# A graph-attention stack for 0/1 edges: softmax weights as products of factors, two graphs interleaved, the general code behind a branch

## Chip, cores, metric

One core of a Trainium2 chip. The metric is the device time of one launch in microseconds (us), the median of several runs; the runs of one kernel mostly agree within about 0.3%, the widest within 0.6%. A "graph" below is one of the 16 graphs of the batch, and the "period" is the time from the end of one graph's output to the end of the next one's. "Clock" is the mean granted TensorE clock of a stretch, as a share of full speed; in the clock records it is 1.00 or 0.50 at any one moment. An engine "stands" when it waits.

## The reference, cut to what matters

```python
# x [16, 1024, 256] float32; adj [16, 1024, 1024] int32 of 0 and 1, symmetric, with a full diagonal
def attend(h, adj, W, a, axis):                  # layers 0 (axis=1) and 1 (axis=-1)
    h = h @ W
    e = leaky_relu((h @ a1)[:, :, None] + (h @ a2)[:, None, :], 0.2)
    return elu(softmax(where(adj > 0, e, -BIG), axis) @ h)

def mean_messages(x, adj):                       # layer 2
    return relu(x @ W_upd + (adj.T @ (x @ W_msg)) / deg + bias)

def heads(x, adj):                               # layer 3: 4 heads of 64 columns
    h = x @ W                                    # per head
    for t in range(5):                           # edge types 1..5
        weight += (adj == t + 1) * (e_src[t][:, None] + e_dst[t][None, :])
    p = softmax(where(adj == 0, -BIG, leaky_relu(weight, 0.01)))
    return layernorm_per_head(relu(p @ h + bias) + h) * gamma + beta

for layer in (attend0, attend1, mean_messages, heads):
    x = x + layer(relu(layernorm(x)), adj)
```

The code allows edge types 1 to 5; the inputs hold only 0 and 1.

## The kernel before

It works on one graph at a time, layer after layer. Layer 3 builds each 128 x 1024 tile of logits from five candidates (one per edge type), takes a row maximum and the exponential, transposes the tile on TensorE, and multiplies.

```python
        def logits(item):                                  # layer 3, one head and one tile of rows
            h, i = item
            # ... kinds[i]: five uint8 masks, one per edge type (made anew for each pair of heads)
            nc.gpsimd.tensor_copy(w, base)
            for t in range(T):                             # T = 5
                nc.scalar.activation(e, ed_rows[h][:, t, :], AF.Identity, bias=hs[:, i, q : q + 1], scale=1.0)
                nc.vector.copy_predicated(w, kind[:, t, :], e)
            nc.vector.scalar_tensor_tensor(w, w, SLOPE3, w, op0=OP.mult, op1=OP.max)
            nc.vector.tensor_reduce(sc[:, 1:2], w, axis=AX.X, op=OP.max, negate=True)

        def attend(item, ready):
            rz = exp_sum(w, *ready)                        # exponential with row sum, on ACT
            pt = transposed(w)                             # 8 transposes on TensorE, 2 copies on ACT
            for n in range(NT):
                nc.tensor.matmul(ps[:, :HO], pt[:, n, :], hs[:, n, cols], start=(n == 0), stop=(n == NT - 1))
            # ... scaling, bias, relu, residual, statistics

    for b in range(B):                                     # one graph behind the other
        adj_n = layer0(b, xs, at); layer1(xs, adj_n); layer2(xs, adj_n)
        # ... next graph's x and first adjacency tiles are loaded here
        layer3(b, xs, adj_n)
```

Of the kernel before, what the change touches and what calls it, by code (L numbers as in the profile page):

```python
# [8 lines left out]
F32 = mybir.dt.float32  # L9
U8 = mybir.dt.uint8  # L10
AF = mybir.ActivationFunctionType
OP = mybir.AluOpType
AX = mybir.AxisListType

P = 128
#: Added to the logits of pairs that have no edge.
NO_EDGE = -1e30


@with_exitstack  # L20
def kernel(
    ctx: ExitStack,
    tc: tile.TileContext,
    x: bass.AP,
# [16 lines left out]
    beta3: bass.AP,  # L41
    out: bass.AP,
):
    """Four graph layers, one graph of the batch after the other, each on chip from its load to its store.

    adj_t is adj with its last two axes swapped; w*_t are the weights with the output axis first.
    a0, a1: [e, 2], the halves of the attention vectors as columns. w3: [d, (h e)]; w3_t: [e, h, d];
    a3: [e, h, 10], source then destination vectors of the five edge types.
    """
    nc = tc.nc  # L50
    B, N, D = x.shape
    NT = N // P
    DC = D // P
    HO, H, T2 = a3.shape
    T = T2 // 2
    HT = H * T
    HALF = 512
    NHALF = N // HALF
# [4 lines left out]
    const = ctx.enter_context(tc.tile_pool(name="const", bufs=1))  # L63
    dram = ctx.enter_context(tc.tile_pool(name="dram", bufs=2, space=bass.MemoryType.DRAM))
    wide_ps = ctx.enter_context(tc.tile_pool(name="wide_ps", bufs=2, space=bass.MemoryType.PSUM))
    tr_ps = ctx.enter_context(tc.tile_pool(name="tr_ps", bufs=2, space=bass.MemoryType.PSUM))
    mm_ps = ctx.enter_context(tc.tile_pool(name="mm_ps", bufs=2, space=bass.MemoryType.PSUM))

# [1 line left out]
    ident = const.tile([P, P], F32)  # L70
    make_identity(nc, ident)
    neg_half = const.tile([P, NT * H], F32)
# [4 lines left out]
        nc.sync.dma_start(t[:, :, :width], src.rearrange("(c p) f -> p c f", p=P))  # L77
        return t

    # Weights with W @ a in the columns behind them, so that one product gives both.  # L80
    wx0 = load_w(w0, D, "wx0", D + 2)
    wx1 = load_w(w1, D, "wx1", D + 2)
    wx2 = load_w(w2_msg, D, "wx2", 2 * D)
    nc.sync.dma_start(wx2[:, :, D:], w2_upd.rearrange("(c p) f -> p c f", p=P))
    wx3 = load_w(w3, D, "wx3", D + HT)
    wd3 = const.tile([P, DC, HT], F32)
    rows = {}
# [4 lines left out]
    with tc.tile_pool(name="prep", bufs=2) as prep:  # L92
        for wt, a, wx in ((w0_t, a0, wx0), (w1_t, a1, wx1)):
            wts = prep.tile([P, DC, D], F32, tag="prep_w", name="wts")
            nc.sync.dma_start(wts, wt.rearrange("(c p) f -> p c f", p=P))
            avs = prep.tile([P, DC, 2], F32, tag="prep_a", name="avs")
# [36 lines left out]
    next_x = load_x(0)  # L133
    next_at = [load_adj(adj_t, 0, n, "adj_t", AHEAD) for n in range(AHEAD)]

# [1 line left out]
    def inv_std(mv, n, eps):  # L137
        """(var + eps) ** -0.5 of n (mean, variance) pairs."""
        rs = small.tile([P, NT * H], F32, tag="rstd", name="rs")
        nc.vector.tensor_scalar(rs[:, :n], mv[:, :n, 1], eps, None, op0=OP.add)  # L140
        nc.gpsimd.tensor_tensor(rs[:, :n], rs[:, :n], neg_half[:, :n], op=OP.pow)  # L141
        return rs

    def norm_relu_t(xs):
        """relu(layernorm(x)), features on the partitions: [P, DC, N]."""
        mv = small.tile([P, NT * H, 2], F32, tag="mv", name="mv")
        for n in range(NT):
            st = small.tile([P, 6], F32, tag="bn", name="st")
            nc.vector.bn_stats(st, xs[:, n, :])
            nc.vector.bn_aggr(mv[:, n, :], st)  # L150
        rs = inv_std(mv, NT, 1e-5)
        ht = state.tile([P, DC, N], F32, name="ht")
        for g in range(NHALF):
            per = NT // NHALF
            pts = [tr_ps.tile([P, HALF], F32, tag="tr", name=f"pt_h{c}") for c in range(DC)]
            for k in range(per):
                n = g * per + k
                hn = work.tile([P, D], F32, name="hn")
                nc.vector.tensor_scalar(hn, xs[:, n, :], mv[:, n, 0:1], rs[:, n : n + 1], op0=OP.subtract, op1=OP.mult)  # L159
                for c in range(DC):  # L160
                    nc.tensor.transpose(pts[c][:, k * P : (k + 1) * P], hn[:, c * P : (c + 1) * P], ident)  # L161
            for c in range(DC):
                nc.scalar.activation(ht[:, c, g * HALF : (g + 1) * HALF], pts[c], AF.Relu)  # L163
        return ht

    def project(ht, wx, n, width):
        """Rows of one node tile times wx, in PSUM."""
        ps = mm_ps.tile([P, HALF], F32, tag="mm", name="ps_proj")
        for c in range(DC):
            nc.tensor.matmul(ps[:, :width], ht[:, c, n * P : (n + 1) * P], wx[:, c, :width], start=(c == 0), stop=(c == DC - 1))  # L170
        return ps
# [6 lines left out]
        return hs  # L178

    def row_everywhere(ht, wx, col):  # L180
        """h @ (W a) of all nodes along the free axis, the same on each partition (PSUM)."""
        ps = wide_ps.tile([P, N], F32, tag="wide", name="ps_row")
        for g in range(NHALF):
            for c in range(DC):
                nc.tensor.matmul(
                    ps[:, g * HALF : (g + 1) * HALF], wx[:, c, col : col + 1].to_broadcast([P, P]),
                    ht[:, c, g * HALF : (g + 1) * HALF], start=(c == 0), stop=(c == DC - 1),
                )
        return ps

    def pipelined(items, first, second):
        """second(item, first(item)) of each item, each behind the next item's first."""
        waiting = None
        for item in items:
            ahead = item, first(item)
            if waiting is not None:
                second(*waiting)
            waiting = ahead
        second(*waiting)

    def edge_logits(row, f, f_s, edges):
        """leaky_relu(row + f) where an edge is, and minus the largest in each row."""
        mask = work.tile([P, N], F32, tag="base", name="mask")
        nc.vector.tensor_scalar(mask, edges, 0.0, NO_EDGE, op0=OP.is_le, op1=OP.mult)
        y = work.tile([P, N], F32, tag="big", name="y", bufs=5)
        nc.scalar.activation(y, row, AF.Identity, bias=f_s, scale=SLOPE)  # L206
        nc.vector.scalar_tensor_tensor(y, row, f, y, op0=OP.add, op1=OP.max)  # L207
        sc = small.tile([P, 4], F32, tag="sc", name="sc", bufs=8)
        nc.vector.tensor_tensor_reduce(y, y, mask, 1.0, -3e38, OP.add, OP.max, sc[:, 0:1])  # L209
        nc.vector.tensor_scalar(sc[:, 1:2], sc[:, 0:1], -1.0, None, op0=OP.mult)  # L210
        return y, sc[:, 1:2], sc

    def exp_sum(out, y, neg_max, sc):
        """out = exp(y - max); returns 1 / its sum over each row."""
        nc.scalar.activation(out, y, AF.Exp, bias=neg_max, scale=1.0, accum_out=sc[:, 2:3])  # L215
        nc.vector.reciprocal(sc[:, 3:4], sc[:, 2:3])
        return sc[:, 3:4]

    def transposed(p):
        """[P, N] -> [P, NT, P]: each block of 128 columns transposed."""  # L220
        pt = work.tile([P, NT, P], F32, tag="big", name="p_t", bufs=5)
        per = HALF // P
        for g in range(NHALF):
            ps = tr_ps.tile([P, HALF], F32, tag="tr", name="ps_t")
            for k in range(per):
                n = g * per + k
                nc.tensor.transpose(ps[:, k * P : (k + 1) * P], p[:, n * P : (n + 1) * P], ident)  # L227
            nc.scalar.copy(pt[:, g * per : (g + 1) * per, :], ps.rearrange("p (k i) -> p k i", i=P))  # L228
        return pt

    def add_elu(v, xs):
        """xs += elu(v)."""
        e = work.tile([P, D], F32, name="e")
        nc.vector.tensor_scalar(e, v, 0.0, None, op0=OP.min)
        nc.scalar.activation(e, e, AF.Exp)
        nc.vector.scalar_tensor_tensor(xs, v, 0.0, xs, op0=OP.max, op1=OP.add)
        nc.vector.scalar_tensor_tensor(xs, e, -1.0, xs, op0=OP.add, op1=OP.add)

# [1 line left out]
    def layer0(b, xs, at):  # L240
        ht = norm_relu_t(xs)
        hs = gat_project(ht, wx0)
# [25 lines left out]
            add_elu(ps[:, :D], xs[:, i, :])  # L268
        return adj_n

# [1 line left out]
    def layer1(xs, adj_n):  # L272
        ht = norm_relu_t(xs)
        hs = gat_project(ht, wx1)
# [17 lines left out]

        pipelined(range(NT), logits, attend)

# [1 line left out]
    def layer2(xs, adj_n):  # L296
        ht = norm_relu_t(xs)
        hs = state.tile([P, NT, D + HT], F32, name="hs")
# [18 lines left out]
            nc.vector.scalar_tensor_tensor(v, ps[:, :D], sc[:, 2:3], up[:, j, :], op0=OP.mult, op1=OP.add)  # L317
            nc.vector.scalar_tensor_tensor(xs[:, j, :], v, 0.0, xs[:, j, :], op0=OP.max, op1=OP.add)

# [1 line left out]
    def layer3(b, xs, adj_n):  # L321
        ht = norm_relu_t(xs)
        # Destination terms of all heads and types, each spread over the partitions by way of DRAM.
        ed = work.tile([HT, N], F32, tag="big", name="ed", bufs=5)
        for g in range(NHALF):
            ps = mm_ps.tile([P, HALF], F32, tag="mm", name="ps_ed")
# [62 lines left out]
        for i in range(NT):  # L389
            for h in range(H):  # L390
                k = i * H + h
# [16 lines left out]
        layer3(b, xs, adj_n)  # L408


# [45 lines left out]
```

## Time and profile before

| before | value |
|---|---|
| time, median of 4 runs | 9663.72 us (9662.92 to 9665.43) |
| one graph | about 604 us, of which layer 3 some 380 |
| DVE busy | 7681 us, 79% of the span, 95% of layer 3 |
| TensorE busy | 5567 us, 58%, at a clock of 0.50 in layer 3 |

The table must be read by layer: DVE bounds layer 3, while layers 0 to 2 are a chain in which engines take turns. One more part of the page, the chain that ended last (shares of the span), says the same: TensorE and DVE share the end, and transfers hold 2% of it.

```profile
PE 42%; DVE 30%; issue 15%; ACT 9%; POOL 2%; DMA 2%; ACTq 0%; SPq 0%; DVEq 0%; POOLq 0%
```

### The profile page before, as it was taken

To read this page: it belongs to the slowest core of one execution; us is meant where nothing else is said; L and a number is where in the kernel's file an instruction comes from. 1 tells how busy PE (TensorE), PEld (TensorE's weight loads), DVE (VectorE), ACT (ScalarE), POOL (GpSimd) and SP (SyncE) were. 2 spreads that over 40 slices of the span, in tenths; PEclk is the share of its full clock that TensorE was granted. 3 is DMA by queue.
4 is the path that set the end of the run, shared out by engine and by line. 5 is a ranking of instruction groups with operands and counts; after the bars stand their busy time and mean duration, and the time that the engine had idled before them with its cause. 6 is when DMAs were issued, how large, how long until landed. Compare 5 with 4: busy or idle time off the path is not lost.

```text
span 9668.2 us, 73868 instructions
## 1 busy us (share of the span) xinstructions
PE 5566.9 (58%) x22944; PEld 4574.6 (47%) x22944; DVE 7681.3 (79%) x13109; ACT 5228.5 (54%) x6785; POOL 1194.6 (12%) x1238
## 2 busy tenths in 40 slices
PE   6456574565745647456475564755647556475564
PEld 5445454454544545445454454544545444454444
DVE  5977959779597795977959779597795977959778
ACT  2745727456374563745637456374563745637456
POOL 1110111101111011110111101011010110101101
PEclk8567585675856758566585665856658566585665
DMA  1110101101111011010110101101011010110000
GB/s 61 51 37 23 44 23 50 37 23 44 32 43 35 23 44 40 35 35 23 44 44 31 35 23 45 43 31 35 23 47 41 33 33 23 47 41 33 22 23 27
DMA packets 85208, 344.25 MB, mean 36 GB/s; under 512 B 8400, under 2 KB 43472, under 8 KB 76624
## 3 DMA queue, kind: packets, MB, share of 16 engines
q1 hardware_dynamic: 47952, 205.29, 5.7%
q0 software_dynamic: 36864, 134.23, 4.8%
q8 instruction: 185, 3.03, 0.1%
q14 instruction: 207, 1.70, 0.1%
HBM read 321.40 MB, written 18.09 MB: 35 GB/s over the span
## 4 chain that ended last, share of the span: by engine, by line
PE 42%; DVE 30%; issue 15%; ACT 9%; POOL 2%; DMA 2%; ACTq 0%; SPq 0%; DVEq 0%; POOLq 0%
PE ps_o L377 17%; PE ps_t L227 9%; DVE w L363 8%; ACT w L215 6%; DVE w L364 6%; DVE sc L366 5%; PE ps_o L288 5%; PE ps_o L264 4%; PE ps_proj L170 3%; DVE res L393 2%; DVE y L207 2%; POOL rs L141 2%; DVE y L209 2%; PE pt_h L161 2%; DMA ed_rows<-ed_d 2%
## 5 line engine op out<-in xcount | busy, mean ns | idle before, releaser
L363 DVE COPY_PREDICATED w<-kind,ps_e 128x1024 f32<-128x1024 uint8 x2560 | 3300.8, 1289 | 210.3 <-ACT ps_e L362 197.2
L362 ACT ACTIVATE ps_e<-ed_rows,hs 128x1024 f32<-128x1024 f32 x2560 | 2861.1, 1118 | 782.8 <-DVE w L363 705.7
L227 PE MATMUL ps_t<-ident,w 128*128 128x128 f32 x4096 | 1007.8, 427 | 2902.3 <-ACT w L215 2902.3
L227 PEld LDWEIGHTS ps_t<-ident,w 128*128 128x128 f32 x4096 | 803.1, 223 | 3002.0 <-ACT w L215 3002.0
L377 PE MATMUL ps_o<-hs,p_t 128*128 128x64 f32 x8192 | 1886.9, 425 | 12.3 <-ACT p_t L228 12.3
L377 PEld LDWEIGHTS ps_o<-hs,p_t 128*128 128x128 f32 x8192 | 1787.5, 330 | 156.7 <-ACT p_t L228 156.7
L215 ACT ACTIVATE w<-w,sc 128x1024 f32<-128x1024 f32 x512 | 587.9, 1148 | 789.9 <-DVE sc L366 789.9
L358 POOL COPY w<-base 128x1024 f32<-128x1024 f32 x512 | 574.2, 1125 | 3461.6 <-PE ps_t L227 3415.5
L163 ACT ACTIVATE ht<-pt_h 128x512 f32<-128x512 f32 x256 | 139.0, 594 | 1361.5 <-PE pt_h L161 1361.4
L354 DVE TENSOR_SCALAR kind<-adj 128x1024 uint8<-128x1024 f32 x1280 | 871.2, 685 | 0.0
L228 ACT COPY p_t<-ps_t 128x512 f32<-128x512 f32 x1280 | 741.9, 582 | 79.0 <-PE ps_t L227 26.3
L264 PE MATMUL ps_o<-hs,p_half 128*128 128x256 f32 x2048 | 570.8, 441 | 271.5 <-DVE sc L210 183.6
L161 PE MATMUL pt_h<-ident,hn 128*128 128x128 f32 x1024 | 295.9, 407 | 700.1 <-DVE hn L159 687.2
L170 PE MATMUL ps_proj<-wx,ht 128*128 128x258 f32 (+2 forms) x2048 | 664.6, 474 | 0.4
L264 PEld LDWEIGHTS ps_o<-hs,p_half 128*128 128x128 f32 x2048 | 439.8, 221 | 409.4 <-ACT y L206 200.5
L364 DVE SCALAR_TENSOR_TENSOR w<-w 128x1024 f32<-128x1024 f32 x512 | 627.1, 1225 | 0.5
L366 DVE TENSOR_REDUCE sc<-w 128x1 f32<-128x1024 f32 x512 | 615.9, 1203 | 0.5
L161 PEld LDWEIGHTS pt_h<-ident,hn 128*128 128x128 f32 x1024 | 168.4, 200 | 904.8 <-issue 637.2
L141 POOL TENSOR_TENSOR rs<-rs,neg_half 128x8 f32<-128x8 f32 (+1 forms) x80 | 192.7, 2409 | 2811.5 <-DVE rs L140 2811.5
L288 PE MATMUL ps_o<-hs,p_t 128*128 128x256 f32 x2048 | 492.8, 395 | 60.3 <-ACT p_t L228 60.3
L159 DVE TENSOR_SCALAR hn<-xs,mv,rs 128x256 f32<-128x256 f32 x512 | 264.5, 544 | 292.8 <-PE pt_h L161 177.4
L170 PEld LDWEIGHTS ps_proj<-wx,ht 128*128 128x128 f32 x2048 | 406.6, 209 | 163.3 <-issue 93.9
(72 smaller groups left out, 6082.8 us busy)
## 6 DMA issues: line engine op xcount, KB each, us to landing
ed_rows<-ed_d SPq DMA_DIRECT2D x64, 2560.0 KB, 8.8
adj_t<-in_adj_t POOLq DMA_DIRECT2D x128, 512.0 KB, 3.9
adj<-in_adj POOLq DMA_DIRECT2D x128, 512.0 KB, 3.9
xs<-in_x SPq DMA_DIRECT2D x16, 1024.0 KB, 5.9
out<-y SPq DMA_DIRECT2D x128, 128.0 KB, 1.7
ed_d<-ed SPq DMA_DIRECT2D x16, 80.0 KB
wx<-in_w SPq DMA_DIRECT2D x3, 256.0 KB, 3.6
wts<-in_w_t SPq DMA_DIRECT2D x2, 256.0 KB
```

Source lines behind the costliest of these rows:

```text
L170: nc.tensor.matmul(ps[:, :width], ht[:, c, n * P : (n + 1) * P], wx[:, c, :width], start=(c == 0), stop=(c == DC - 1))
L215: nc.scalar.activation(out, y, AF.Exp, bias=neg_max, scale=1.0, accum_out=sc[:, 2:3])
L227: nc.tensor.transpose(ps[:, k * P : (k + 1) * P], p[:, n * P : (n + 1) * P], ident)
L228: nc.scalar.copy(pt[:, g * per : (g + 1) * per, :], ps.rearrange("p (k i) -> p k i", i=P))
L264: nc.tensor.matmul(ps[:, :D], p_halves[n // per][:, n % per, i * P : (i + 1) * P], hs[:, n, :D], start=(n == 0), stop=(n == NT - 1),)
L288: nc.tensor.matmul(ps[:, :D], pt[:, n, :], hs[:, n, :D], start=(n == 0), stop=(n == NT - 1))
L354: nc.vector.tensor_scalar(kind[:, t, :], adj_n[i], float(t + 1), None, op0=OP.is_equal)
L362: nc.scalar.activation(e, ed_rows[h][:, t, :], AF.Identity, bias=hs[:, i, q : q + 1], scale=1.0)
L363: nc.vector.copy_predicated(w, kind[:, t, :], e)
L364: nc.vector.scalar_tensor_tensor(w, w, SLOPE3, w, op0=OP.mult, op1=OP.max)
L366: nc.vector.tensor_reduce(sc[:, 1:2], w, axis=AX.X, op=OP.max, negate=True)
L377: nc.tensor.matmul(ps[:, :HO], pt[:, n, :], hs[:, n, cols], start=(n == 0), stop=(n == NT - 1))
```

## The change

The intent has four parts.

1. Factors. With one edge type, exp(leaky(s + d)) = max(exp(s) exp(d), exp(a s) exp(a d)). Up to a factor that cancels in the softmax, one tile of weights is one DVE operation on a row and a column of exponentials and the 0/1 mask. No maximum, no wide exponential, no predicated copies.
2. Layout. The tile is made in the layout in which TensorE takes its weights, so the transposes of weights go. Row sums come from a column of ones in the product.
3. Layer 2 in float32r (a second 32-bit type for products), its messages split into a high part, which is the cast to that type, and a low part, which is what the cast leaves.
4. Two graphs interleaved. The code of a graph is a generator; a list orders the pieces of two graphs that stand 105 units apart (units are the numbers that the pieces yield in the code below). The engines take their queues in order, so this order decides what lies beside what.

A check at the end (sums of squares of the adjacency, sums of edges, size of the logit terms) decides by a branch whether the general code, which is the whole kernel before, runs as well.

```diff
-def tile_gnn_stack_kernel(
+def tile_general_stack(              # the whole kernel before, unchanged in what it does
 ...
+def tile_simple_stack(ctx, tc, flag, x, adj, adj_t, ...):
+    def layer3(b, xs, mask):
+        ht = norm_relu_t(xs)
+        # ... 8 projections into hs, logit terms into `terms`
+        yield 11
+        d_row = spread(column(terms[:, :, :H], H), H, (S3 - 1.0,), "l3")     # exp of terms -> DRAM
+        # ... q = exp((1 - S3) * terms); hb = (hs + bias) * exp(S3 * terms), on GpSimd
+        for h in range(H):
+            row = everywhere(d_row[h], "row3")                               # DRAM -> 128 partitions
+            for g in range(NHALF):
+                for j in range(NT):
+                    p = work.tile([P, HALF], F32, tag="p3", name="p3", bufs=14)
+                    nc.vector.scalar_tensor_tensor(
+                        p, row[:, half], q[:, j, h : h + 1], mask[:, j, half], op0=OP.max, op1=OP.mult)
+                    yield 0.2
+                for k in range(PER):
+                    for j in range(NT):
+                        nc.tensor.matmul(ps[:, k * HW : (k + 1) * HW],
+                            ps_[j][:, k * P : (k + 1) * P], hbv[:, j, h, :], start=(j == 0), stop=(j == NT - 1))
+                yield 5.4
+        for i in range(NT):
+            # ... normalisation per head on DVE, GpSimd (power) and ACT
+            nc.gpsimd.tensor_tensor(y, of, rows["gamma3"], op=OP.mult)
+            nc.gpsimd.tensor_tensor(y, y, rows["beta3"], op=OP.add)
+            nc.gpsimd.tensor_tensor(y, y, xs[:, i, :], op=OP.add)
+            nc.sync.dma_start(out[b, i * P : (i + 1) * P, :], y)
+            yield 0.5
+    # ... layers 0, 1, 2 in the same way; layer 0 makes a tile with two DVE operations
+    APART = 105.0
+    queue = [(b * APART, b, graph(b)) for b in range(B)]
+    while queue:                                   # the piece that is due first is emitted next
+        queue.sort(key=lambda g: g[:2])
+        at, b, g = queue.pop(0)
+        step = next(g, None)
+        if step is not None:
+            queue.append((at + step, b, g))
+    # ... the check, which counts what does not fit into `flag`
+    tile_simple_stack(tc, flag, *args)
+    again = nc.values_load(flag[0:1, 0:1], ...)
+    with tc.If(again > 0):
+        tile_general_stack(tc, *args)
```

## The prediction

> **What bounds the kernel now.** I read the page's totals first, then the slices, then busy time cut by layer for the first graph, then the costly groups, then single bursts in the timeline.
>
> ```profile
> PE 5566.9 (58%) x22944; PEld 4574.6 (47%) x22944; DVE 7681.3 (79%) x13109; ACT 5228.5 (54%) x6785; POOL 1194.6 (12%) x1238
> ...
> PE   6456574565745647456475564755647556475564
> ...
> DVE  5977959779597795977959779597795977959778
> ...
> PEclk8567585675856758566585665856658566585665
> ```
> DVE is the busiest engine, but its digits swing between 5 and 9: a mean over unlike layers. Busy us by engine in the layers of graph 0 (load, layers 0, 1, 2, start of 3, layer 3):
> ```profile
> 35.00:110.00 75.00, 52.51 (x184) 38.92 (x184) 50.15 (x117) 26.65 (x44) 14.78 (x15) 0.83 0.31 98
> 110.00:180.00 70.00, 53.80 (x250) 42.74 (x251) 43.21 (x101) 37.09 (x68) 1.64 (x1) 0.89 0.00 0
> 180.00:220.00 40.00, 39.44 (x143) 27.03 (x142) 16.09 (x49) 5.15 (x12) 0.00 (x0) 0.91 0.00 1
> 220.00:260.00 40.00, 23.73 (x91) 14.93 (x89) 17.09 (x36) 9.67 (x16) 4.71 (x4) 0.86 0.34 133
> 260.00:640.00 380.00, 180.16 (x778) 163.38 (x779) 361.67 (x533) 249.25 (x286) 62.96 (x65) 0.50 0.09 31
> ```
> Columns: stretch, length, PE, PEld, DVE, ACT, POOL, then the clock. Layer 3 takes some 380 of a graph's 604 us (9668/16); DVE is busy 95% of it and the clock is 0.50 because TensorE mostly waits. Layers 0 to 2 have no full engine but TensorE in layer 2: phases follow one another. The groups behind it:
> ```profile
> L363 DVE COPY_PREDICATED w<-kind,ps_e 128x1024 f32<-128x1024 uint8 x2560 | 3300.8, 1289 | 210.3 <-ACT ps_e L362 197.2
> L362 ACT ACTIVATE ps_e<-ed_rows,hs 128x1024 f32<-128x1024 f32 x2560 | 2861.1, 1118 | 782.8 <-DVE w L363 705.7
> ...
> L377 PE MATMUL ps_o<-hs,p_t 128*128 128x64 f32 x8192 | 1886.9, 425 | 12.3 <-ACT p_t L228 12.3
> ...
> L354 DVE TENSOR_SCALAR kind<-adj 128x1024 uint8<-128x1024 f32 x1280 | 871.2, 685 | 0.0
> ...
> L364 DVE SCALAR_TENSOR_TENSOR w<-w 128x1024 f32<-128x1024 f32 x512 | 627.1, 1225 | 0.5
> ```
> Five predicated copies per head and tile, one per edge type, make 43% of DVE's work. Bursts that give unit costs (transposes cold and warm, layer 3's products cold, layer 2's warm, two GpSimd rows):
> ```profile
> 429.65 1.97 PE L227 MATMUL ps_t<-ident,w 128*128 128x128 f32 x8 [5.36 <-ACT w L215]
> ```
> ```profile
> 139.10 1.04 PE L227 MATMUL ps_t<-ident,y 128*128 128x128 f32 x8
> ```
> ```profile
> 431.50 3.68 PE L377 MATMUL ps_o<-hs,p_t 128*128 128x64 f32 x16
> ```
> ```profile
> 199.54 27.90 PE L308 MATMUL ps_o<-hs,adj 128*128 128x257 f32 x128
> ```
> ```profile
> 618.03 0.73 POOL L395 TENSOR_TENSOR y<-res,row_gamma 128x256 f32<-128x256 f32 x1 [1.10 <-DVE res L393]
> ```
> ```profile
> 230.03 1.64 POOL L141 TENSOR_TENSOR rs<-rs,neg_half 128x8 f32<-128x8 f32 x1 [50.89 <-DVE rs L140]
> ```
>
> **What the Trainium skill says.** "TensorE: Matmul & The Clock Gate", section "What's actually happening", gives 1.2 GHz after idleness and 2.4 when busy; the trace agrees (clock 0.50 in layer 3; transposes 1.97 against 1.04). "FP8 and Floating Point Precision", "TensorE Precision Notes": true FP32 takes four passes. The trace agrees: a product shows as two records, and 128 records of 257 columns take 27.90 us, 0.218 each, two clocks per column. "VectorE: DVE Perf Modes", "Mode 2×_2P": fp32 tensor_scalar gets double rate, two-tensor operations do not; the trace agrees (685 ns against 1225 for 1024 elements). "Advanced Engine Details and Errata", "DVE Details" and "GPSIMD Details": the Pool engine shares an interface with DVE and conflicts when DVE has two SBUF inputs; nothing before isolates that. I found no page on float32r's rate.
>
> **The change, part by part.** With one edge type, exp(leaky(s+d)) is a maximum of two products of exponentials, so a tile of weights is one DVE operation (two in layer 0), already in the layout TensorE needs. All predicated copies, kind masks, row maxima, wide exponentials and transposes of weights go.
>
> TensorE per graph, full clock: 64 transposes x 0.107 (half of 1.97/8 = 0.246, less drain) = 7; projections, two of 258 columns (32 records x 0.218 = 7 each), one of 512 (32 x 0.43 = 14), one of 264 (7) = 35; layers 0 and 1, 128 records x 0.218 = 28 each. Layer 2 becomes 64 products with a high part and 64 with a low one in float32r: an estimate of one clock per column (0.108) gives 14. Layer 3 keeps 256 products, 512 records. Before, 16 took 3.68 less some 0.15 of drain, 0.22 each at half clock, set by the weight load (3.49 for 16); at full clock 0.107 to 0.11: 55. Sum 167 us, times 16 = 2,670.
>
> DVE per graph, consecutive operations starting about 0.08 earlier than durations suggest (1225 becomes 1.14): normalisations 32 x 0.39 + 1.5 = 14; layer 0 8 x 2.7 (two wide operations, reciprocal, scaling) + 16 x 0.38 = 28; layer 1 8 x 1.15 + 8 x 1.0 = 17; layer 2 16 x 0.42 + 8 x 1.15 = 16; layer 3 64 half-width x 0.62 = 40, output 8 x 1.95 = 16, copies and small ones 4. Sum 135, times 16 = 2,160, against 7,681. ACT about 70 a graph, GpSimd about 75. So TensorE becomes the fullest engine, but not alone.
>
> What interleaving hides I read from the queue orders of the built program, since each engine runs its queue in order. In a steady period (one graph), graph b ends layer 3 while b+1 ends layer 1; then b+1 does layer 2 with layer 0 of b+2; then b+1's layer 3 with b+2's layer 1.
> 1. Output of layer 3: on GpSimd eight rounds of three 256-wide operations (2.4 measured, 618.03 to 620.43) plus one power of four columns (about 1.0, by the slope from 1647 ns for 8 to 5457 for 32), plus mask loads: 30 us. On TensorE only 24 layer-1 products (10.4) lie beside it, and the last elementwise work of layer 1 is queued on DVE among this output. x has two buffers, so b+2's load waits for the end of the output.
> 2. Layer 2 projection, load and normalisation of b+2, its projection, row out to DRAM and back (about 7), then eight DVE rounds of 2.7 mixed with layer 2's ends (6): about 60 us from the output's end to the last weight tile, for 42 of TensorE work. Adjacency has 8 buffers for 16 half-tiles, so the second half loads behind the first half's products.
> 3. Then TensorE is full: 56 products of layer 0 (24), layer 3's projection (9), layer 3 (55), layer 1's projection (9), 40 products of layer 1 (17): 114.
> 4. Clock ramps after gaps and the start of layer 1's weights: about 7.
> Sum 211 us a graph. First output ends at about 360 (start 25, layers 0 and 1 nearly alone 140, then parts 2, 3, 1); 14 more periods, 2,954; last graph's layers 2 and 3 alone, and the check, about 150. That is 3,464. I place the prediction slightly lower, 3,400, as I counted some overlaps as serial.
>
> **Rivals.**
> - TensorE bound throughout, phase gaps hidden: 2,670 plus 100 to 150 for the ends, about 2,800. For it: two graphs have 334 us of TensorE work, more than one's own chain. Against it: in-order queues put both graphs' waiting phases (parts 1 and 2) side by side, and x's second buffer ties them.
> - DVE and GpSimd slow each other: almost every new DVE operation has two SBUF inputs. If GpSimd's 45 us of elementwise work per graph held DVE up for its length, the period would be 225 to 245 and the time 3,700 to 4,000.
> - float32r at FP32's rate: layer 2 takes 55 instead of 14, partly in part 2's slack: 20 to 40 a graph more, 3,750 to 4,050.
> - The check fails and the general code runs as well: about 13,000. Against it: adjacency is 0/1, symmetric, with a diagonal; degrees of at most 1024 are exact in both sums; the logit terms, sums of 256 products of order 0.1, should stay far under 30.
>
> **Range and chances.** All rivals but the last are at least twice as fast. 3,050 needs 20 us less a graph (output hidden, weight load at 0.09); 3,800 needs 25 more. Faster 0.985, same 0.005, slower 0.01.
>
> **What would show it.** Right: PE busy about 2,700 us, 78% of the span; DVE about 2,200; clock mostly 0.9 or more; layer-3 pairs at 0.11 us; dips of PE and full GpSimd once per period near 210 us; the longest TensorE waits in the transposes after layer 1 and in layer 0's products waiting for weights. Wrong: wide two-input DVE operations well over 1.2 us (port), 258-column float32r records near 0.2 or above, a clock near 0.5 in layer 3, or lines of the old code running after the check.

## The result, and the profile after

| | before | after |
|---|---|---|
| time, median of 4 runs each | 9663.72 us | 3831.82 us (3828.86 to 3833.42) |
| ratio | 1 | 0.3965 (0.3959 to 0.397) |

A ratio here is the mean time of one kernel's fast runs over that of the other's fast runs of the same rounds, so it is not quite the ratio of the medians.

The direction and the order of size are as predicted. The time is not: 3,832 us lies 432 us above the predicted 3,400 and 32 us above the top of the range. The page of the changed kernel, its totals and some of its slices:

```profile
PE 3033.8 (79%) x17490; PEld 2610.1 (68%) x17490; DVE 2277.1 (59%) x6389; ACT 1101.9 (29%) x2769; POOL 1059.5 (28%) x1366
...
PE   4778796877968778797877968779697877968785
...
POOL 1123314142132323214142132323314142132312
PEclk8899898989989889898888989899898989989865
```

DVE's work fell from 7,681 to 2,277 us, and TensorE is the fullest engine at 79%, close to the predicted 78%. But 79% of 3,830 us is 3,034 us of busy time, where 2,700 was predicted: work and time both came out an eighth larger, so the share agrees by luck. PE's dips still come once a period, and GpSimd is fullest in them. The last two digits of the clock, 6 and 5, are new: they come to matter below.

The groups that answer to the predicated copies of before, with busy time and mean of one:

```profile
L753 PE MATMUL ps_o<-hs,p 128*128 128x65 f32 x8192 | 1015.0, 286 | 107.4 <-DVE p L745 107.3
L745 DVE SCALAR_TENSOR_TENSOR p<-row,q,mask 128x512 f32<-128x512 f32 x1024 | 718.7, 759 | 358.1 <-PE ps_o L753 294.1
...
L559 PE MATMUL pt_h<-ident,hn 128*128 128x128 f32 x1024 | 206.1, 307 | 331.4 <-ACT hn L557 331.4
```

Layer 3's weights now cost DVE 719 us in all. The longest wait of TensorE is that of the transposes (331 us, most of it before layer 2, 18.3 a graph), as the prediction said; the wait for layer 3's first weights (107 us, 6.7 a graph) was not in its sum.

One period cut at the prediction's three parts. Columns: stretch, length, then busy time and count of PE, PEld, DVE, ACT, POOL, then the clock, DMA share and GB/s. The first line is part 1 (output of layer 3), then part 2 (to the last layer-0 weight tile), then part 3.

```profile
1513.30:1542.90 29.60, 11.30 (x52) 9.37 (x51) 21.14 (x98) 15.23 (x40) 25.36 (x30) 0.74 0.27 83
1542.90:1609.60 66.70, 50.13 (x221) 36.01 (x219) 36.80 (x103) 20.65 (x47) 9.11 (x15) 0.83 0.31 97
1609.60:1744.80 135.20, 124.75 (x818) 114.31 (x818) 83.36 (x198) 33.01 (x87) 31.35 (x41) 0.95 0.13 40
```

GpSimd fills 25.4 of part 1's 29.6 us; in part 3 TensorE is busy 92%. In part 2 nothing is full, which is the mark of a chain from engine to engine. The last GpSimd operation of the first graph's output and of the fifteenth's:

```profile
392.07 0.72 POOL L780 TENSOR_TENSOR y<-y,xs 128x256 f32<-128x256 f32 x1
```
```profile
3606.32 0.72 POOL L780 TENSOR_TENSOR y<-y,xs 128x256 f32<-128x256 f32 x1
```

(3,606.32 - 392.07) / 14 = 229.6 us a period, against 211. The prediction's own sum, before it was shaded, compares with the trace so:

| term of the sum | predicted | measured | excess |
|---|---|---|---|
| to the end of the first output | 360 | 393 | 33 |
| part 1 of a period | 30 | 29.6 | 0 |
| part 2 | 60 | 66.7 | 6.7 |
| part 3, ramps and start of layer 1 (114 + 7) | 121 | 135.2 | 14.2 |
| 14 periods (mean 229.6) | 2,954 | 3,214 | 260 |
| last graph alone, and the check | 150 | 223 | 73 |
| sum | 3,464 | 3,830 | 366 |
| shaded down to | 3,400 | | 64 more |

The three parts are those of the period shown, 231.5 us. Over twelve steady periods of the trace their means are 29.6, 64.9 and 135.2 us.

Three questions follow: what the last graph loses, what the 19 us a period are, and whether any rival (instruction cost of the branch, DVE and GpSimd on one port, float32r's rate) has a share in them.

### The profile page after: what moved, and what is told of

Same layout as the page of the kernel before. It is cut to its first block, busy times and chain, and to the rows that moved or that the text cites. A ratio compares the mean times of both kernels' runs of the same rounds, so it can differ in the third digit from the quotient of the medians.

```text
span 3829.6 us, 48243 instructions
## 1 busy us (share of the span) xinstructions
PE 3033.8 (79%) x17490; PEld 2610.1 (68%) x17490; DVE 2277.1 (59%) x6389; ACT 1101.9 (29%) x2769; POOL 1059.5 (28%) x1366
## 5 line engine op out<-in xcount | busy, mean ns | idle before, releaser
L753 PEld LDWEIGHTS ps_o<-hs,p 128*128 128x128 f32 x8192 | 1022.7, 204 | 128.3 <-issue 113.9
L753 PE MATMUL ps_o<-hs,p 128*128 128x65 f32 x8192 | 1015.0, 286 | 107.4 <-DVE p L745 107.3
L745 DVE SCALAR_TENSOR_TENSOR p<-row,q,mask 128x512 f32<-128x512 f32 x1024 | 718.7, 759 | 358.1 <-PE ps_o L753 294.1
L632 PE MATMUL ps_o<-hs,p 128*128 128x256 f32 x2048 | 529.9, 403 | 97.4 <-DVE hs L626 78.3
L665 PE MATMUL ps_o<-hs,p 128*128 128x257 f32 x2048 | 493.2, 399 | 40.4 <-DVE p L659 40.4
L632 PEld LDWEIGHTS ps_o<-hs,p 128*128 128x128 f32 x2048 | 389.5, 200 | 162.3 <-DVE hs L626 79.2
L665 PEld LDWEIGHTS ps_o<-hs,p 128*128 128x128 f32 x2048 | 398.2, 199 | 110.3 <-issue 54.9
L538 POOL TENSOR_TENSOR rs<-rs,neg_half 128x4 f32<-128x4 f32 (+1 forms) x192 | 238.6, 1244 | 835.3 <-DVE rs L537 817.0
L703 PE MATMUL ps_o<-hi,adj 128*128 128x258 f32 x1024 | 308.3, 329 | 121.9 <-DVE v L710 118.4
L557 ACT ACTIVATE hn<-xs,shift,rs 128x256 f32<-128x256 f32 x512 | 288.8, 598 | 217.7 <-DVE shift L550 167.0
L703 PEld LDWEIGHTS ps_o<-hi,adj 128*128 128x128 f32 x1024 | 230.9, 226 | 132.8 <-issue 127.8
L704 PE MATMUL ps_o<-lo,adj 128*128 128x258 f32 x1024 | 298.4, 320 | 0.0
L546 DVE BATCH_NORM_STATS2 st<-xs 128x6 f32<-128x256 f32 x512 | 204.7, 409 | 126.9 <-DMA xs<-in_x 123.8
```

Source lines behind the costliest of these rows:

```text
L538: nc.gpsimd.tensor_tensor(rs[:, :n], rs[:, :n], neg_half[:, :n], op=OP.pow)
L546: nc.vector.bn_stats(st, xs[:, n, :])
L557: nc.scalar.activation(hn, xs[:, n, :], AF.Relu, bias=shift[:, n : n + 1], scale=rs[:, n : n + 1])
L632: nc.tensor.matmul(ps[:, :D], ps_[j][:, i * P : (i + 1) * P], hs[:, j, :D], start=(j == 0), stop=(j == NT - 1))
L665: nc.tensor.matmul(ps[:, : D + 1], ps_[j][:, i * P : (i + 1) * P], hs[:, j, : D + 1], start=(j == 0), stop=(j == NT - 1),)
L703: nc.tensor.matmul(ps[:, : D + 2], a, hi[:, i, :], start=(i == 0), stop=False)
```

## The experiments

Where no other number is named, differences are against 3,831.8 us. Runs with two or four timings each.

### The branch and the general code behind it

```diff
-    with tc.If(again > 0):
-        tile_general_stack(tc, *args)
```

> The general code and its branch are left out; the 0/1 path alone runs. My theory (the time is sixteen in-order periods of about 230 us): 3,815 to 3,830 us, at most some 10 us less than the changed kernel, as nothing of the general code runs. Rival (the larger program costs time throughout, by instruction fetch): more than 40 us less.

Measured 3,827.67 us, 4 less, which lies within the spread of the runs. The code that isn't run costs nothing worth naming.

### The last graph's layer 3

In the tail TensorE is busy and slow at the same time. Windows of the kernel after: layer 3 of the last graph, then its output, then the check and the end.

```profile
3689.00:3787.00 98.00, 97.48 (x457) 97.30 (x457) 36.67 (x78) 3.56 (x10) 2.02 (x2) 0.50 0.03 12
3787.00:3818.00 31.00, 0.00 (x0) 0.00 (x0) 17.84 (x76) 10.82 (x31) 25.00 (x30) 0.50 0.09 31
3818.00:3830.00 12.00, 0.00 (x0) 0.00 (x0) 0.00 (x0) 0.00 (x0) 0.00 (x0) 0.50 0.04 14
```

For 98 us TensorE and its weight loads are busy 99%, yet the clock stands at 0.50, and 457 records take 0.214 us each. In a steady period the same products take 0.111. There, wide products of the other graph stand between them; here nothing does. If the clock is all that differs, then a few wide products ahead of the stream should lift it:

```diff
+        if b == B - 1:
+            for w in range(3):
+                ps = mm_ps.tile([P, HALF], F32, tag="mm", name="ps_warm")
+                for c in range(NT):                       # 128 x 512 products, result unused
+                    nc.tensor.matmul(ps, ht[:, 0, :P], ht[:, 0, :HALF], start=(c == 0), stop=(c == NT - 1))
         for h in range(H):
             row = everywhere(d_row[h], "row3")
```

> 24 extra 512-column FP32 products (result unused) before layer 3 of the last graph only. Theory (in the last graph layer 3's stream runs at half clock because it starts after a gap, and a stream bound by weight loads doesn't release the clock by itself): its 512 records go from 0.214 to 0.111 us and the span falls by 35 to 50 us, to about 3,785. Rival (such a stream can't hold the full clock): records back at 0.214 after a few us, span unchanged or up to 10 us longer.

Measured 3,789.33 us, 42 less. The trace of this run, a window inside the same stage and the run of products:

```profile
3690.00:3750.00 60.00, 58.12 (x516) 57.49 (x514) 37.96 (x82) 4.93 (x14) 2.42 (x3) 0.99 0.06 19
```
```profile
3706.14 41.98 PE L758 MATMUL ps_o<-hs,p 128*128 128x65 f32 x374
```

Same products, nearly the same busy share (97%), clock 0.99 in place of 0.50, 0.112 us a record (41.98 / 374) in place of 0.214. So the stream of narrow products, each with its own 128 columns of weights to load, stayed at the clock at which it began, high or low, for 40 to 100 us. This settles 42 us of the 73.

### One graph behind the other

```diff
-    APART = 105.0
+    APART = 1000.0
```

> Graphs one after the other instead of two interleaved, same operations. My theory: one graph alone takes about 135 us for layers 0 and 1 (25 to 160 us in the trace) and about 208 for layers 2 and 3 with its output (last graph), so 16 x 330 to 345 = 5,300 to 5,500 us; the factor form gives about 4,250 of the 5,830 us gained and the interleaving about 1,550. Rival (TensorE's work sets the time, interleaving matters little): below 4,300 us.

Measured 5,460.49 us. One period of it:

```profile
641.00:982.00 341.00, 248.53 (x1109) 216.12 (x1109) 148.96 (x402) 70.21 (x174) 65.89 (x85) 0.70 0.13 42
```

TensorE works 248.5 us a graph here, against 186.2 in the period of the interleaved kernel shown above, for the same products. The clock is 0.70, and layer 3 is at half speed in every graph. To see how much of interleaving's gain is filled gaps and how much is the clock, the same serial kernel got 16 wide products ahead of every layer 3:

```diff
-    APART = 105.0
+    APART = 1000.0
+        for w in range(2):      # in layer 3 of every graph: 2 x 8 wide products, as above
```

> Graphs one after the other as in e2_serial, with 16 wide FP32 products (result unused) ahead of layer 3 in every graph. Theory (without interleaving layer 3 runs at half clock, and much of what interleaving gives is the clock that the other graph's wide products keep up, not the filled gaps): layer 3's stream takes 57 instead of 112 us a graph, the wide products cost some 7 beyond a wait that is there anyway: 16 x 45 to 50 less, 4,660 to 4,750 us. Rival (the clock falls back, or interleaving's gain is filled gaps alone): above 5,350 us.

Measured 4,683.47 us, 777 less than the serial kernel, 49 a graph. All 512 records of a layer 3 now run as one stretch:

```profile
3137.40 57.28 PE L758 MATMUL ps_o<-hs,p 128*128 128x65 f32 x512
```

Interleaving takes 5,460 to 3,832, a gain of 1,629 us. 777 of them, near half, can be had by the clock of layer 3 alone, without overlapping two graphs. In the clock records layer 3's stream stays at 0.50 in all 16 graphs of the serial kernel and at 1.00 in all 16 of this one. That the interleaved kernel's own gain divides in the same way is not shown; its TensorE is busy 921 us less than the serial one's (3,955 to 3,034), so the clock counts there too. The prediction had counted interleaving as overlap only.

### Part 1: the output of layer 3

If GpSimd's rounds bound part 1, then taking one of its three operations out of each round shortens the period. Beta is added to x beforehand, in layer 3, where GpSimd has time:

```diff
+            if h == 1:
+                for i in range(NT):
+                    nc.gpsimd.tensor_tensor(xs[:, i, :], xs[:, i, :], rows["beta3"], op=OP.add)
 ...
             nc.gpsimd.tensor_tensor(y, of, rows["gamma3"], op=OP.mult)
-            nc.gpsimd.tensor_tensor(y, y, rows["beta3"], op=OP.add)
             nc.gpsimd.tensor_tensor(y, y, xs[:, i, :], op=OP.add)
```

> The addition of beta moves from the output's rounds on GpSimd to layer 3's start (GpSimd is idle there), so a round on GpSimd has two 256-wide operations instead of three. Theory (GpSimd's rounds set the length of part 1): eight times 0.8 us = 6 us less a period, 3,730 to 3,750 us in all. Rival (DVE or ACT set it, or the wait moves on to the load of x and the masks): less than 2 us a period, above 3,800 us.

Measured 3,773.64 us: 58 less, 3.6 a period where 6 were expected. Part 1 went from 29.6 to 25.0 us in the mean of twelve periods. So GpSimd's rounds do bear on part 1, but of the 6 us taken out of them not all was gained; what holds the rest wasn't isolated. The number lies between what the two theories expected.

The edit changed a second thing. DVE's main operation of these rounds, with its shortest, median and longest duration in ns, in the kernel after and in this run:

```profile
L766 DVE SCALAR_TENSOR_TENSOR o<-o,hs x128: 413/830/952, 353.9 to 3808.7; 128x256 f32<-128x256 f32 x128
```
```profile
L768 DVE SCALAR_TENSOR_TENSOR o<-o,hs x128: 395/424/841, 354.3 to 3749.8; 128x256 f32<-128x256 f32 x128
```

It is slow where GpSimd works beside it (see the rivals below), and that became rarer. The 58 us hold both effects; no run separates them.

### Part 2: the weights of layer 0

If part 2 ends with DVE's eight rounds for layer 0, then one wide operation less per tile is worth its full duration.

```diff
-            nc.vector.scalar_tensor_tensor(p, row_a, q[:, j : j + 1], row_b, op0=OP.mult, op1=OP.max)
-            nc.vector.scalar_tensor_tensor(p, p, 1.0, mask[:, j, :], op0=OP.mult, op1=OP.mult, accum_out=z[:, 0:1])
+            nc.vector.scalar_tensor_tensor(p, row_a, q[:, j : j + 1], mask[:, j, :], op0=OP.mult, op1=OP.mult, accum_out=z[:, 0:1])
```

> Wrong result on purpose: layer 0's weights take one wide DVE operation instead of two (the maximum is left out). Theory (part 2 ends when DVE has made layer 0's eight weight tiles): 8 x 1.2 = 10 us less a period, 3,660 to 3,700 us in all. Rival (part 2 is set by layer 2's adjacency loads, the row's trip through DRAM or by TensorE): less than 3 us a period, above 3,785 us.

Measured 3,680.15 us: 152 less, 9.5 a period (its two runs lie 21 us apart, 1.3 a period). That would be 8 x 1.19 us, but the edit also drops the wait for the second of the two rows. In the kernel after and in this run, from the transpose that starts the row's trip to the first weight operation:

```profile
1577.34 0.27 PE L579 MATMUL ps_col<-ident,col 128*8 128x128 f32 x1
```
```profile
1514.62 0.27 PE L579 MATMUL ps_col<-ident,col 128*8 128x128 f32 x1
...
1520.77 1.28 DVE L623 SCALAR_TENSOR_TENSOR p<-row,q,mask 128x1024 f32<-128x1024 f32 x1
```

That is 6.2 us here where it was 7.4 (to 1584.74, next fence), and 1.4 less in the mean of 15 graphs. So some 8 of the 9.5 us are the rounds, near what was taken out of them. In the trace of the kernel after, the rounds begin when the row comes back from DRAM and run without a stop to the end of part 2:

```profile
1584.74 2.48 DVE L622 SCALAR_TENSOR_TENSOR p<-row,q 128x1024 f32<-128x1024 f32 x2 [1.18 <-DMA row<-d_row]
...
1607.80 1.22 DVE L624 SCALAR_TENSOR_TENSOR p<-p,mask 128x1024 f32<-128x1024 f32 x1
```

That is 24.3 us for eight rounds with layer 2's ends among them; 8 x 2.7 + 6 = 27.6 was predicted. So part 2's excess lies before the row: 41.8 us from the output's end to 1584.74, where 60 - 27.6 = 32.4 was left. The trace has a stand there that nobody had counted, ACT behind a mask load that GpSimd, with its one staging buffer, issued only after the output and the load of x:

```profile
1552.88 1.06 ACT L527 ACTIVATE mask<-raw 128x1024 uint8<-128x1024 int32 x1 [4.16 <-DMA raw<-in_adj_t]
```

It isn't the only one. DVE stands longer, for the next graph's x, whose statistics are queued on it ahead of `lo` and `up` of layer 2 (the low part of the messages, and the update with its bias). TensorE's projections of layer 2 then wait for `up`:

```profile
1551.62 0.75 DVE L546 BATCH_NORM_STATS2 st<-xs 128x6 f32<-128x256 f32 x2 [10.28 <-DMA xs<-in_x]
...
1553.39 0.42 DVE L696 TENSOR_TENSOR up<-ps_proj,row_bias 128x256 f32<-128x256 f32 x1
```
```profile
1553.96 2.98 PE L566 MATMUL ps_proj<-wx,ht 128*128 128x512 f32 x4 [3.49 <-DVE up L696]
```

DVE's stands for x come to 123.8 us in 15 graphs. The prediction had the load of x in this part ("b+2's load waits for the end of the output"). The runs that follow were aimed at ACT's stand alone; none moves the load of x, so this rival is untested.

### Mask loads earlier: three misses

A second staging buffer for the masks, paid with two of the 14 buffers of layer 3's weights:

```diff
-        raw = work.tile([P, N], I32, tag="raw", name="raw", bufs=1)
+        raw = work.tile([P, N], I32, tag="raw", name="raw", bufs=2)
 ...
-                    p = work.tile([P, HALF], F32, tag="p3", name="p3", bufs=14)
+                    p = work.tile([P, HALF], F32, tag="p3", name="p3", bufs=12)
```

> Two landing buffers instead of one for the adjacency rows that ACT turns into the mask (layer 3's weight buffers go from 14 to 12 to make room). Theory (in part 2 ACT stands in order behind a mask load for 4 us, and normalisation and projection stand behind ACT): 3 to 5 us less a period, 3,750 to 3,785 us. Rival (that wait lies beside another one, DVE's weights): within 1% of the changed kernel, above 3,800 us.

Measured 3,891.56 us, 60 more: a miss. ACT's stands behind mask loads fell from 85 to 20 us in all, but the loads and ACT's mask operations moved into part 1, among the output's rounds, and the wait that ends part 1 grew. The transposes of layer 2's input, in the kernel after and in this one:

```profile
1542.02 1.18 PE L559 MATMUL pt_h<-ident,hn 128*128 128x128 f32 x4 [18.30 <-ACT hn L557]
```
```profile
1566.91 1.18 PE L559 MATMUL pt_h<-ident,hn 128*128 128x128 f32 x4 [23.94 <-ACT hn L557]
```

5.6 us a period more before these transposes: time won behind the output was paid in front of it. In means of twelve periods part 1 grew by 4.6 us, part 2 fell by 2.0 (DVE still stands 118 us for x), and part 3 grew by 1.1, which the two weight buffers fewer may have cost. Two more runs put the mask loads on another issuing engine, with beta moved and 16 wide products ahead of the last layer 3 (the two gains found so far); the third is the same without moved loads, as the yardstick.

```diff
-        nc.gpsimd.dma_start(raw, adj_t[b, n * P : (n + 1) * P, :])
+        nc.sync.dma_start(raw, adj_t[b, n * P : (n + 1) * P, :])      # the other run: nc.scalar
```

> e5_out2 and e4_warm together, and the mask loads issued from SyncE's queue instead of GpSimd's. Theory (GpSimd's rounds in part 1 are the bound, mask issues cost 0.65 us each there, and the output's dependence on them falls): 2 to 4 us a period below the two combined (3,732), 3,680 to 3,705 us. Rival (SyncE's queue then holds rows or stores behind a mask load that waits for ACT): above 3,740 us.

> As c1_sync with the mask loads issued from ACT's queue. Theory: as c1_sync, 3,680 to 3,705 us. Rival (issuing on ACT delays its activations by about as much): 3,725 us or more.

> e5_out2 and e4_warm together, mask loads as in the changed kernel. The two act in different places, so their gains add: 3,774 less 42, 3,725 to 3,740 us. Rival (they overlap): 3,755 or more.

Measured 3,755.26 (SyncE), 3,809.58 (ACT) and, with the loads left on GpSimd, 3,721.9 us. Both moves lose, as the rivals expected; whether for the rivals' reasons was not looked at. TensorE's wait before the transposes is 276.8 us in all in the yardstick, 325.5 with SyncE and 322.1 with ACT, some 3 us a graph more, as with the second buffer. The gains of beta and of the wide products add: 58 + 42 = 100 expected, 110 measured; 16 wide products in place of 24 cost 14.0 us in the trace and not 20.9. What of part 2's excess is the mask load's stand stays open, since each way of shortening it lengthened the wait ahead of the transposes.

### Distance between the graphs, and wide products in the gap

```diff
-    APART = 105.0
+    APART = 115.0
```

> The second graph is emitted 10 units later against the first (115 instead of 105), so that more of layer 1's wide products come during the other graph's output. Theory (part 1 leaves TensorE idle for 18 us because too few of layer 1's products are left for it): some 5 to 10 us less a period, 3,670 to 3,760 us, unless the shift opens a gap elsewhere. Rival (sum of gaps is fixed by the chain of one graph's own waits): within 1%.

Measured 3,923.63 us, 92 more: a miss. TensorE's busy time rose from 3,034 to 3,177 us for the same products, and the clock of the run fell from 0.883 to 0.854: with another order more products ran at the low clock, those of layer 3 were busy for 1,096 us in all (1,015 before) and those of layer 1 for 548 (493). I had weighed waits and not the clock. That the lower clock cost the 92 us is argued and not shown by a run of its own.

```diff
+        for w in range(2):              # layer 2, ahead of the transposes: 16 wide products
+            ps = mm_ps.tile([P, HALF], F32, tag="mm", name="ps_fill")
+            for c in range(NT):
+                nc.tensor.matmul(ps, ident, xs[:, 6:8, :], start=(c == 0), stop=(c == NT - 1))
         ht = norm_relu_t(xs)
```

> 16 wide FP32 products (result unused) per graph in the gap between layer 1's last product and layer 2's transposes; they read the rows that layer 1 finished last, so they run just before the transposes. Theory (each period pays a few us for restarting at half clock there): 2 to 4 us less a period, 3,765 to 3,800 us. Rival (the restart lies beside DVE's and ACT's chain, or the products are in the way): within 0.5% or slower.

Measured 3,937.58 us, 106 more: a miss, and the rival's result ("the products are in the way"). The filler began only when the last elementwise work of layer 1 had freed x:

```profile
1571.80 16.91 PE L688 MATMUL ps_fill<-xs,ident 128*128 128x512 f32 x32 [7.78 <-DVE xs L678]
...
1588.55 0.60 PE L559 MATMUL pt_h<-ident,hn 128*128 128x128 f32 x4
```

A record of 512 columns at full clock takes 0.43 in a burst (the prediction's unit cost), here 0.53: a part of the filler was itself at low speed (its first 3.2 us ran at a clock of 0.50). From the end of layer 1's products to the transposes it is now 24.5 us (1,564.0 to 1,588.55) where it was 18.3. In these runs warming up paid only where TensorE would otherwise have stood.

### Part 3: the row's trip before layer 3

The first weights of layer 3 need a row of exponentials that goes to DRAM and comes back on all partitions. TensorE stands meanwhile, and then starts at half clock (kernel after; the second number of a line is the length of the burst):

```profile
1405.17 0.27 PE L579 MATMUL ps_col<-ident,col 128*32 128x128 f32 x1
1412.07 0.66 PE L753 MATMUL ps_o<-hs,p 128*128 128x65 f32 x2 [6.62 <-DVE p L745]
1412.53 1.16 PE L632 MATMUL ps_o<-hs,p 128*128 128x256 f32 x2
...
1418.85 5.69 PE L753 MATMUL ps_o<-hs,p 128*128 128x65 f32 x50
```

A kernel with wrong weights in one head takes the first row from a tile on chip:

```diff
-            row = everywhere(d_row[h], "row3")
+            row = everywhere(d_row[h], "row3") if h else xs[:, 0:4, :].rearrange("p a b -> p (a b)")
```

> Wrong result on purpose: the row of head 0 in layer 3 is taken from a tile that is already on chip, so the first weights of layer 3 no longer wait for the row's trip through DRAM. Theory: the 6.6 us for which TensorE stands before the first layer-3 product of each graph are on the path that sets the period (part 3 is full of TensorE work, nothing else fills the hole). Then the period falls by 5 to 6.6 us and the time is 3,725 to 3,755 us. Rival: something else (the weights that DVE makes, GpSimd's rounds before) ends just as late and takes the wait's place; then less than half is gained and the time stays over 3,785.

Measured 3,809.45 us, only 22 less, 1.4 a period: the rival's number. (The comparison let one head's wrong weights through.) The trace says what took the wait's place:

```profile
1394.48 1.34 PE L753 MATMUL ps_o<-hs,p 128*128 128x65 f32 x10
1396.44 0.41 PE L753 MATMUL ps_o<-hs,p 128*128 128x65 f32 x2 [0.61 <-DVE p L745]
1397.46 0.41 PE L753 MATMUL ps_o<-hs,p 128*128 128x65 f32 x2 [0.61 <-DVE p L745]
1398.12 8.66 PE L753 MATMUL ps_o<-hs,p 128*128 128x65 f32 x50 [0.26 <-DVE p L745]
```

TensorE now meets DVE's pace, tile by tile, with short stands and no wide product in between; and the stream runs partly at half clock, 8.66 us for 50 records against 5.69. Its busy time in layer 3 rose by 50 us in all. The clock fell during this stream, which had begun at full speed:

```profile
1398.00:1400.00 2.00, 1.88 (x17) 1.91 (x18) 2.00 (x5) 0.00 (x0) 0.00 (x0) 1.00 0.97 266
...
1402.00:1404.00 2.00, 2.00 (x11) 2.00 (x11) 0.78 (x2) 0.00 (x0) 0.00 (x0) 0.50 0.00 0
```

So narrow products kept their clock in the last graph, where they ran without stands, and lost it here, behind a row of short ones. A stand was swapped for slow work. The other way is to fill the trip with work that is there anyway. The transposes for the row and the trip are issued one group of the other graph's layer-0 products earlier:

```diff
-        yield 11
+        yield 7
         watch(b, 2, terms)
         d_row = spread(column(terms[:, :, :H], H), H, (S3 - 1.0,), "l3")
+        row_0 = everywhere(d_row[0], "row3")
+        yield 4
 ...
-            row = everywhere(d_row[h], "row3")
+            row = everywhere(d_row[h], "row3") if h else row_0
```

> A correct version: the transposes of the terms and the row's trip are issued before one more group of eight layer-0 products of the other graph (about 3.5 us of TensorE work) instead of after it, so that this work lies inside the trip. If the trip is on the path, about 3 us a period are gained: 3,775 to 3,795 us. If it is not, as before: 3,820 to 3,840.

Measured 3,770.66 us, 61 less, 3.8 a period. The group lies inside the trip, half of the wait is left, and the products behind it run at full clock:

```profile
1372.85 0.27 PE L579 MATMUL ps_col<-ident,col 128*32 128x128 f32 x1
1372.96 3.62 PE L632 MATMUL ps_o<-hs,p 128*128 128x256 f32 x16
1379.93 0.41 PE L755 MATMUL ps_o<-hs,p 128*128 128x65 f32 x2 [3.35 <-DVE p L747]
...
1381.26 0.65 PE L632 MATMUL ps_o<-hs,p 128*128 128x256 f32 x2
```

A burst of two wide records took 1.16 us behind the long stand and 0.65 behind the short one. So the trip is on the path, and what it costs is the stand together with the clock after it.

### The version that beats both kernels

Beta moved, 16 wide products ahead of the last layer 3, and the row early:

> The early row together with the two gains found before (beta added to x on GpSimd ahead of layer 3's output, wide dummy products ahead of the last layer 3), which alone stood at 3,722 us. If the gains add, 3,665 to 3,690 us; if the shorter output part already moved the wait elsewhere, 3,700 to 3,725.

Measured 3,668.12 us (3,656.72 to 3,674.25, 4 runs), correct; its ratio to the kernel before is 0.3798 (0.3791 to 0.3804), where the changed kernel had 0.3965. The three gains add: 58 + 42 + 61 = 161 expected, 164 measured.

## Why the prediction was right or wrong

**What held.** DVE's work falls to near 2,200 us and TensorE becomes the fullest engine: 2,277 us and 79%. The period has the three parts that were read from the queue orders. Part 1 is 29.6 us for 30, and GpSimd's rounds bear on it (one of its three operations was worth 3.6 us a period, the easing of DVE included). Part 2 ends with DVE's layer-0 tiles (one operation of each was worth some 8 us a period). Layer 3's records take 0.111 us in a steady period. The TensorE waits named beforehand, for the transposes and for layer 0's weights, are in the list of waits at 331 and 78 us in all, though two others (for layer 2's sums, 118, and layer 3's weights, 107) are longer than the second. The general code didn't run.

**The rivals.** "TensorE bound throughout, 2,800" fell: waits of one graph do stand beside waits of the other. Float32r at FP32's rate fell. These are products of 258 columns, high and low part in turn; they start 0.12 us apart:

```profile
1579.61 0.28 PE L703 MATMUL ps_o<-hi,adj 128*128 128x258 f32 x1
1579.73 0.28 PE L704 MATMUL ps_o<-lo,adj 128*128 128x258 f32 x1
```

That is the prediction's estimate of 0.108 us, plus a tenth. In the second half of layer 2 they start 0.215 apart, which was named as a sign against the estimate, but TensorE is at half clock there:

```profile
1590.00:1599.00 9.00, 7.64 (x33) 7.40 (x34) 9.00 (x23) 0.00 (x0) 0.00 (x0) 0.50 0.01 4
```

"DVE and GpSimd slow each other" gave a period of 225 to 245 and a time of 3,700 to 4,000, and the measured period, 229.6, lies inside. The slowing is real, but much smaller than this rival had it. Sorted in the trace of the kernel after by whether GpSimd did arithmetic beside them, the 33 output operations of L766 without it took 418 ns in the median and the 95 others 832. Of layer 3's weight operations 949 took 747 ns and the 75 others 976:

```profile
L745 DVE SCALAR_TENSOR_TENSOR p<-row,q,mask x1024: 718/747/979, 261.5 to 3770.6; 128x512 f32<-128x512 f32 x171
```

Over all DVE operations with two inputs this makes some 84 us, 5.2 a graph, where the rival let it reach GpSimd's 45. The sign that the prediction had named, wide operations well over 1.2 us, couldn't show it: they took 1.20 to 1.30 us in layer 0, but no GpSimd arithmetic ran beside them. What the 5.2 us are worth in the period is not isolated. A right number from a rival is not the rival's proof.

**The step that failed first** is "I place the prediction slightly lower, 3,400, as I counted some overlaps as serial." Nothing in the profile said so; the sum stood at 3,464, and each of its terms turned out equal or too small. This step is 64 of the 432 us; the terms below are the rest. A list made from a trace holds the waits that one has seen. What it lacks only adds time.

**The terms that were mis-sized** (part 3 is the largest, 14.2 us in each of 14 periods):

- "3. Then TensorE is full: ... 114", with 7 more for ramps: 121 predicted, 135.2 measured. The row's trip before layer 3 was missing: a stand of 6.6 us, then some 7 us at half clock. Issuing the row earlier gave 3.8 back. TensorE's busy time in the part is 124.8 and not 114: 2.0 us are layer 2's last 16 records, which the prediction had placed in part 2; half clock explains at most 6.8 (the clock was 0.95 over 135.2 us, so 13.5 of them at half), about what the 7 us for ramps had allowed for. How the rest divides I didn't isolate.
- "2. ... about 60 us": 66.7 measured in the period shown, 64.9 in the mean. DVE's rounds were shorter than predicted (24.3 for 27.6), the way to them longer (41.8 for 32.4). Two stands lie in it, DVE's for x (10.3 us, a load that the prediction had named) and ACT's behind a mask load (4.2 us). Which of them is the excess was not shown: every way of moving the mask loads cost more than it gave, and the load of x was not moved.
- "last graph's layers 2 and 3 alone, and the check, about 150": 223 measured. It took layer 3 at full clock, because TensorE would be busy. It ran at half clock, alone and behind a stand of 6.4 us, and 24 wide products ahead of it gave 42 us back. The other 31 us weren't looked into.
- "first output ends at about 360": 393 measured. Its own terms, 25 + 140 + 60 + 121 + 30, make 376, so 16 of the 33 us are a slip in the sum. The other 17 weren't looked into.

**Behind the last graph's term stands one idea that was wrong**: that a TensorE without gaps has a full clock. The prediction put the clock of 0.50 in the old layer 3 down to TensorE's waits; in the last graph it was 0.50 with TensorE busy 99%. In the prediction the clock entered as 7 us of ramps. In the runs it is a second thing that the interleaving buys (777 of its 1,629 us can be had by the clock alone), and what a rearrangement of the queue puts at risk: with the distance of 115 and with the row on chip TensorE was busy 143 and 68 us longer for the same products.

**The range.** Its top, 3,800, was "25 us more a graph" than 3,400. With 3,464 as the middle and the same width up and down it would have reached 3,864 and held the result; it was drawn around the shaded number.

## What to carry to other kernels

Take the sum that the steps give and leave it; if anything is to be shaded, upwards, for waits that the trace of the old kernel cannot show. When a change reorders a queue, follow the TensorE clock as an own term: a stream of narrow products with a weight load each kept the speed at which it started here where it ran without stands (42 and 57 us at 0.99 to 1.00, 98 us at 0.50), so put wide products ahead of it, and fill a wait with wide work from elsewhere rather than shorten it to a row of small stands, behind which such a stream lost its clock. A load moved out of one wait lands in another stage; ask what that stage was short of.

## What the Trainium skill lacked or had wrong

- "TensorE: Matmul & The Clock Gate", section "What's actually happening", has the full clock come after about 3.4 us of sustained work. Here 457 records of 65 columns, with TensorE and its weight loads busy 99%, stayed at a clock of 0.50 for 98 us (0.214 us a record), and the same stream behind 24 wide products held 0.99 (0.112). Which measure of activity counts for such narrow products, the page doesn't say; busy time in the profile isn't it.
- No page has float32r's rate on TensorE: 258 columns took 0.12 us from start to start at full clock, where an FP32 product of 257 columns takes two records of 0.22.
